# A two-layer graph network on one core: the halves of x written to DRAM in the first pass of layer 1 and loaded in the three later ones

## The chip, the core and the metric

The kernel runs on one core of one Trainium2 chip. The metric is the device time of one execution in microseconds (us). The core has a matrix engine (TensorE, PE in the profile; PEld is its weight load), a vector engine (DVE), a scalar engine (ACT), a general engine (GpSimd, POOL) and a queue engine (SyncE, SP). SP, ACT and POOL issue transfers between DRAM and on-chip memory; sixteen DMA engines carry them all.

## The reference: what is computed

There are 6250 nodes with 256 features and 100000 edges, sorted by target node. The targets are drawn as the square of a uniform number, so that low-numbered nodes have many more edges. Both layers sum the rows of the sources of a node's edges, add the node's own row, and send the result through two matrix products with ReLU. At the end x is added and each row is normalised.

```python
def _gin_agg(h, src, dst, eps, n_nodes):
    agg = jax.ops.segment_sum(h[src], dst, num_segments=n_nodes)
    return (1.0 + eps) * h + agg
...
h = _gin_agg(x, src, dst, eps1, n)
h = jax.nn.relu(h @ W1a + b1a)
h = jax.nn.relu(h @ W1b + b1b)
h = _gin_agg(h, src, dst, eps2, n)
h = jax.nn.relu(h @ W2a + b2a)
out = h @ W2b + b2b
...
x = _layernorm(x + out, axis=-1)
```

W1a is 256x512, W1b and W2a are 512x512, W2b is 512x256. Everything is float32.

## The kernel before, in words

The 6250 nodes are 49 tiles of 128 rows; the last has 106. The 100000 edges are 782 chunks of 128. A short preparation transposes the edge lists onto the partitions and makes index tables; then layer 1 writes its result `h1` (`h` in the profile) to DRAM, and layer 2 gathers from it.

**Two ways of summing edges.** In each layer the edges of most nodes are summed by *gathers*: POOL issues one indirect DMA for a chunk of 128 edges (line 461), which brings 128 rows into a buffer called `early` (in layer 2 also `late`). There are 494 such gathers in each layer. Four gathers are a piece, and the buffer holds six pieces in layer 1, so that piece i+6 can only be gathered once the sums of piece i are done. The sums are matmuls with a matrix of zeros and ones, one matmul for each gather (line 954), mostly two pieces at a time; they are copied to `split` by ACT (line 982), placed by another matmul (line 1001) and added to a tile's accumulator `acc` by DVE (line 1011). The accumulators are seeded with the tile's own rows by SP's loads (line 866) and scaled by ACT (line 883).

The lowest seven tiles (0 to 6, the *heavy* ones, 288 chunks) are done without gathers. For them layer 1 counts, for each pair of a heavy node and a source, how many edges join the two: DVE makes zero-one tiles `cb` and `ca` (lines 1532 and 1523), PE multiplies them (line 1571), and DVE adds the result to a table `at` (line 1594). Then the sums are dense products of counts with x.

**The passes over x.** `first_products` makes these products in layer 1. Their float32 precision is had by splitting x into two halves, the value rounded to the matrix engine's faster format and what is left. It goes over all of x four times: for tiles 6 and 5, 4 and 3, 2 and 1, and 0. A pass has 13 *ranges* of four tiles (the last range has one). For each range of each pass

- SP loads the range of x into a tile `raw` (`in_rows`, line 1188; 512 KB, two buffers),
- ACT rounds it into the upper half of a tile `xh` (line 1385) and copies it to PSUM in two parts (line 1392), from which DVE subtracts the upper half to make the lower one (line 1394). `xh` has two buffers,
- ACT turns the counts of each heavy tile into `cf` (line 1415), and makes and stores a 16-bit copy `ci` to DRAM for layer 2 (lines 1423 and 1428),
- PE multiplies `cf` with `xh` and adds up in one PSUM bank for each heavy tile (line 1457, four matmuls for a range and tile).

When a tile's accumulator is complete, PE transposes it (line 1047), and the two products follow (line 1086 with `w1a_s`, line 1115 with `w1b_s`); ACT evaluates the first ReLU (line 1096) and the last (line 1127), and issues the store of the result (line 1128).

**Who sets the order.** All engines run in the order in which the program is written, and a planner in the kernel (class `Plan`) sets that order: it plays the work through with assumed costs for PE, DVE and ACT, assumed times for loads (`LOAD` is 6 us), and buffers that are taken and released (`Room`). Each step of work is a Python generator that asks the planner for a buffer, for an event or for an engine, and its instructions are written at the moment the engine is granted. The order is fixed at build time; on the chip each instruction waits on semaphores for what it needs. SP's queue in layer 1 holds the loads of `raw` and of the accumulators, in the order in which the planner let them start; behind them stand the loads of layer 2.

Layer 2 has the same structure with 512 features, without the counting: it reads the 16-bit counts back (line 1243), loads `h1` as `xr`, splits it, and multiplies (line 1331).

Of the kernel before, what the change touches and what calls it, by code (L numbers as in the profile page):

```python
# [10 lines left out]
F32 = mybir.dt.float32  # L11
I32 = mybir.dt.int32
F32R = mybir.dt.float32r
# [4 lines left out]
P = 128  # L18
# [8 lines left out]
W = 10  # L27
RANGE = 4
# [133 lines left out]
GATHERS = (1.28, 1.265)  # L162
LANDINGS = (5.0, 6.0)
LOAD = 6.0
SEEDS = (6.0, 12.0)
WHOLE = 16.0
COUNTS = 12.0
# [15 lines left out]
def act(n):  # L183
    return 0.12 + 0.00083 * n
# [152 lines left out]
def tile_gin_residual_layernorm(  # L337
# [38 lines left out]
    nc = tc.nc  # L376
    N, D = x.shape
# [3 lines left out]
    NT = -(-N // P)  # L381
    NCH = -(-E // P)
    NC, taken = counted(N, E, HEAVY[0])
    STEPS, END, PASSES, FREE = steps(N, E, taken, HEAVY[0])
# [97 lines left out]
    with tc.tile_pool(name="prep", bufs=2) as prep, tc.tile_pool(  # L482
        name="prepp", bufs=2, space=bass.MemoryType.PSUM
# [30 lines left out]
        rest = E - full * P  # L514
# [44 lines left out]
        for i, c in enumerate(range(NC2, NCP, 512)):  # L559
            n = min(512, NCP - c)  # L560
# [6 lines left out]
        for g0, g1 in runs:  # L567
            c, h = groups[g0]
            n = g1 - g0
# [156 lines left out]
    def rows(t):  # L726
        return min(P, N - t * P)
# [25 lines left out]
    def ordered(ctx):  # L753
        odram = ctx.enter_context(
            tc.tile_pool(name="odram", bufs=1, space=bass.MemoryType.DRAM)
        )

        ctx.enter_context(tc.manual_schedule())

        ranges = [range(k, min(k + RANGE, NT)) for k in range(0, NT, RANGE)]  # L760
        counts = odram.tile([len(ranges), HEAVY[1], P, RANGE * P], mybir.dt.uint16, name="counts")

        def layer(number, ctx, table, width, scale, weights, ba, wide):
# [6 lines left out]
            loan = ctx.enter_context(tc.tile_pool(name=f"loan{number}", bufs=1))  # L770
# [7 lines left out]
            plan = Plan(BEGINS[number - 1], {"PE": FREES[number - 1], "DVE": FREES[number - 1],  # L778
                                             "ACT": FREES[number - 1]}, NEXT[number - 1])
# [392 lines left out]
            def whole_rows(ks):  # L1172

                return min(len(ks), N // P - ks[0])

            def in_rows(ks, to, of):

                n = whole_rows(ks)
                some = []
                if n:  # L1180
                    some.append((
                        to[:, :n],
                        of[ks[0] * P : (ks[0] + n) * P].rearrange("(k p) d -> p k d", p=P),
                    ))
                if n < len(ks):
                    some.append((to[: rows(ks[n]), n], of[ks[n] * P : N]))
                for a, b in some:
                    nc.sync.dma_start(a, b)
# [167 lines left out]
                    cleared[ts].more(sum(t >= RING for t in ts) * len(ranges))  # L1356

            def first_products():
                xh_room = Tiles(loan, [P, RANGE, 2, width], F32R, "xh", 2)
                raw_room = Tiles(loan, [P, RANGE, width], F32, "raw", 2)  # L1360
                ci_room = Tiles(loan, [P, RANGE * P], mybir.dt.uint16, "ci", 2)
                xh_of = {}
                turns = [(ts, r) for ts in PASSES for r in range(len(ranges))]
                halved = {k: Event(plan) for k in turns}
                made = {(t, r): Event(plan) for ts, r in turns for t in ts}
                factors = {}

                def loading():
                    yield ("rest", 80.0)
                    for ts, r in turns:  # L1370
                        raw = yield ("get", raw_room, 0)
                        in_rows(ranges[r], raw.tile, table)
                        token = yield ("get", xh_room, 0)
                        xh_of[ts, r] = token
                        plan.start(halving(ts, r, token.tile, raw))

                def halving(ts, r, xh, raw):
                    ks = ranges[r]
                    yield ("rest", LOAD)
                    n = whole_rows(ks)  # L1380
                    for m, js in ((P, slice(0, n)), (rows(NT - 1), slice(n, len(ks)))):
                        if js.start < js.stop:
                            c = (js.stop - js.start) * width
                            yield ("on", "ACT", act(c), 1)
                            nc.scalar.copy(xh[:m, js, 0, :], raw.tile[:m, js, :])
                            for j in range(js.start, js.stop, 2):
                                two = slice(j, min(j + 2, js.stop))
                                token = yield ("get", banks, 2)
                                c = (two.stop - j) * width
                                yield ("on", "ACT", act(c), 1)  # L1390
                                ap = bank[token.number][:m, :c].rearrange("p (k d) -> p k d", d=width)
                                nc.scalar.copy(ap, raw.tile[:m, two, :])
                                yield ("on", "DVE", dve(c), 1)
                                nc.vector.tensor_tensor(  # L1394
                                    xh[:m, two, 1, :], ap, xh[:m, two, 0, :], op=ALU.subtract
                                )
                                token.release()
                    raw.release()
                    plan.then(halved[ts, r].set)

                def factoring():
                    for ts in PASSES:
# [37 lines left out]
                def multiplying():  # L1440
                    for ts in PASSES:
                        tokens = []
                        for t in ts:
                            wanted[block_of[t]].set()
                        for r, ks in enumerate(ranges):
                            for t in ts:
                                yield ("until", made[t, r])
                            yield ("until", halved[ts, r])
                            for t in ts:
                                if r == 0:  # L1450
                                    tokens.append((yield ("get", banks, 3)))
                            yield ("on", "PE", 0.3 + 0.235 * len(ks) * len(ts), 1)
                            for i, t in enumerate(ts):
                                cf, xh = factors[t, r].tile, xh_of[ts, r].tile
                                for j, k in enumerate(ks):
                                    m = rows(k)
                                    nc.tensor.matmul(  # L1457
                                        bank[tokens[i].number][:, : 2 * width], cf[:m, j, :],
                                        xh[:m, j, :, :].rearrange("p a d -> p (a d)"),
                                        start=(k == 0), stop=(k == NT - 1),  # L1460
                                    )
                                factors[t, r].used()
                            xh_of[ts, r].release()
                        for t, token in zip(ts, tokens):
                            plan.then(plan.start, adding(t, token))

# [14 lines left out]
            def counting():  # L1481
# [1 line left out]


                F16 = mybir.dt.float16
                cb_room = Tiles(loan, [P, NT * W], F16, "cb", 10)
                ca_room = Tiles(loan, [P, BATCH, P], F16, "ca", 4)
                yield ("on", "DVE", 2.5, 4)
                si = loan.tile([P, NC], I32, tag="si", name="si")
# [399 lines left out]
```

## Time and profile before

| what | value |
|---|---|
| three timed runs | 1334.89, 1335.60, 1339.82 us (median 1335.60) |
| the profiled execution's own time | 1333.73 us |
| its span, first to last instruction | 1332.0 us |
| PE, DVE, ACT, POOL busy | 1171.7, 872.8, 603.2, 963.8 us |
| bytes moved by DMA | 305.72 MB, mean 230 GB/s |
| last gather of layer 1 / first of layer 2 issued at | 650.16 / 676.63 us |

All durations come from the profiled execution; its span is 1.7 us shorter than its own time. A line such as `L1394 DVE TENSOR_TENSOR xh<-bank,xh 128x512 ... x96 | 65.1, 684` says that the instructions of line 1394 run on DVE, write `xh` from `bank` and `xh`, stood in the span 96 times, were busy 65.1 us and took 684 ns each; behind the next bar stands how long the engine had been idle just before them, and what ended that. A queue name with a q (SPq) means the engine's issuing of a transfer, not the transfer.

### The profile page before, as it was taken

To read this page: it belongs to the slowest core of one execution; us is meant where nothing else is said; L and a number is where in the kernel's file an instruction comes from. 1 tells how busy PE (TensorE), PEld (TensorE's weight loads), DVE (VectorE), ACT (ScalarE), POOL (GpSimd) and SP (SyncE) were. 2 spreads that over 40 slices of the span, in tenths; PEclk is the share of its full clock that TensorE was granted. 3 is DMA by queue.
4 is the path that set the end of the run, shared out by engine and by line. 5 is a ranking of instruction groups with operands and counts; after the bars stand their busy time and mean duration, and the time that the engine had idled before them with its cause. 6 is when DMAs were issued, how large, how long until landed. Compare 5 with 4: busy or idle time off the path is not lost. (4 is left out here: it accounts for less than half of the span.)

```text
span 1332.0 us, 18717 instructions
## 1 busy us (share of the span) xinstructions
PE 1171.7 (88%) x6027; PEld 756.0 (57%) x6027; DVE 872.8 (66%) x2031; ACT 603.2 (45%) x1118; POOL 963.8 (72%) x1002
## 2 busy tenths in 40 slices
PE   2379888999899999878759899999989999999986
PEld 1145554655454655444436667767667766677755
DVE  7689888697897787323127668777756655653443
ACT  0213677767675763454255354334334433432222
POOL 6877777777777777777457677777777777777770
PEclk8589999999999999968879899999989999999999
DMA  3635666667676775566669889888889999877782
GB/s 103 189 119 178 182 219 198 207 199 227 207 225 188 219 239 170 151 211 193 198 228 333 296 268 310 252 278 287 289 271 309 301 310 301 289 244 240 242 244 69
DMA packets 160860, 305.72 MB, mean 230 GB/s; under 512 B 25672, under 2 KB 93150, under 8 KB 160754
## 3 DMA queue, kind: packets, MB, share of 16 engines
q0 software_dynamic: 63232, 194.31, 47.2%
q1 hardware_dynamic: 75110, 84.23, 19.3%
q10 hardware_dynamic: 22412, 25.89, 5.6%
q8 instruction: 51, 0.84, 0.3%
q14 instruction: 55, 0.45, 0.1%
HBM read 273.90 MB, written 30.44 MB: 228 GB/s over the span
## 5 line engine op out<-in xcount | busy, mean ns | idle before, releaser
L461 POOL DMA_INDIRECT early<-in_x_dram,srcs x494 | 488.9, 990 | 158.9 <-issue 127.4
L461 POOL DMA_INDIRECT early<-h,srcs x250 | 239.8, 959 | 101.4 <-issue 58.8
L461 POOL DMA_INDIRECT late<-h,srcs x244 | 232.5, 953 | 77.6 <-issue 60.2
L1011 DVE SCALAR_TENSOR_TENSOR acc<-bank,mask,acc 128x256 f32<-128x256 f32 (+1 forms) x368 | 212.8, 607 | 39.4 <-PE bank L1001 34.8
L1086 PE MATMUL bank<-zt,w2a_s 128*128 128x256 f32 (+2 forms) x864 | 181.8, 366 | 7.7 <-DVE acc L1011 6.5
L1115 PE MATMUL bank<-w1b_s,ht 128*128 128x512 f32 (+1 forms) x392 | 184.7, 599 | 1.1 <-DVE acc L1011 0.8
L1086 PEld LDWEIGHTS bank<-zt,w2a_s 128*128 128x128 f32 x864 | 154.8, 195 | 30.4 <-DVE acc L1011 6.9
L954 PE MATMUL bank<-early,sel 128*32 128x256 f32 (+1 forms) x1488 | 134.3, 475 | 32.7 <-DMA early<-h,srcs 15.3
L1331 PE MATMUL bank<-upper,cf 128*128 128x512 f32 (+1 forms) x343 | 149.2, 435 | 13.9 <-ACT upper L1220 13.5
L1331 PE MATMUL bank<-xr,cf 128*128 128x512 f32 (+1 forms) x343 | 138.2, 403 | 0.8 <-DVE xr L1225 0.8
L1594 DVE TENSOR_TENSOR at<-bank,at 128x490 f32 x174 | 115.9, 666 | 28.2 <-ACT cf L1415 14.7
L907 DVE TENSOR_TENSOR sel<-iota,slot 128x256 f32<-128x256 f32 (+2 forms) x116 | 50.6, 436 | 123.5 <-PE bank L954 119.5
L1086 PE MATMUL bank<-zt,w1a_s 128*128 128x256 f32 (+2 forms) x432 | 103.2, 389 | 13.7 <-ACT zt L1059 10.4
L1001 PE MATMUL bank<-split,to 128*128 128x256 f32 (+2 forms) x340 | 100.0, 415 | 15.6 <-ACT split L987 8.7
L1115 PEld LDWEIGHTS bank<-w1b_s,ht 128*128 128x128 f32 (+1 forms) x392 | 73.3, 191 | 70.8 <-issue 58.6
L1457 PE MATMUL bank<-xh,cf 128*128 128x512 f32 (+1 forms) x343 | 104.1, 440 | 8.7 <-DVE xh L1394 8.6
L1255 ACT CAST cf<-ci 128x512 fp32r<-128x512 uint16 (+1 forms) x91 | 53.8, 595 | 121.4 <-PE bank L1331 104.3
L1096 ACT ACTIVATE ht<-bank,b2a_s 128x256 f32<-128x256 f32 (+2 forms) x108 | 44.6, 451 | 139.5 <-PE bank L1086 137.0
L954 PEld LDWEIGHTS bank<-early,sel 128*32 128x32 f32 x1488 | 40.0, 112 | 113.4 <-issue 80.2
L1571 PE MATMUL bank<-cb,ca 128*128 128x490 f16 x288 | 87.6, 381 | 16.1 <-DVE at L1594 10.5
L1115 PE MATMUL bank<-w2b_s,ht 128*128 128x256 f32 (+1 forms) x392 | 101.5, 390 | 0.0
L1086 PEld LDWEIGHTS bank<-zt,w1a_s 128*128 128x128 f32 x432 | 81.9, 207 | 32.7 <-ACT zt L1059 14.9
(138 smaller groups left out, 1650.7 us busy)
## 6 DMA issues: line engine op xcount, KB each, us to landing
raw<-in_x_dram SPq DMA_DIRECT2D x48, 512.0 KB, 4.5
h<-h1r ACTq DMA_DIRECT2D x48, 256.0 KB, 2.5
xr<-h SPq DMA_DIRECT2D x12, 1024.0 KB, 7.3
counts<-ci ACTq DMA_DIRECT2D x84, 128.0 KB, 3.4
ci<-counts SPq DMA_DIRECT2D x84, 128.0 KB, 5.0
acc<-h SPq DMA_DIRECT2D x19, 512.0 KB, 7.5
early<-in_x_dram,srcs POOLq DMA_INDIRECT x494
acc<-in_x_dram SPq DMA_DIRECT2D x21, 256.0 KB, 3.9
```

Source lines behind the costliest of these rows:

```text
L461: nc.gpsimd.indirect_dma_start(out=rows_[:, j, :], out_offset=None, in_=table, in_offset=bass.IndirectOffsetOnAxis(ap=srcs[:, c : c + 1], ...
L907: nc.vector.tensor_tensor(sel[:, :n, :], iota[:, :SLOTS].unsqueeze(1).to_broadcast([P, n, SLOTS]), slot[:, c0 : c0 + n].unsqueeze(2).to_br ...
L954: mm = nc.tensor.matmul(pm[b * SLOTS : (b + 1) * SLOTS], sel[:, c - groups[g][0], :], rows_[:, l, :], start=(c == part[0]), stop=(c == par ...
L1001: nc.tensor.matmul(pu[:, i * width : (i + 1) * width], to[:used], split[:used, l, :], start=(once or l == 0), stop=(once or l == 1),)
L1011: nc.vector.scalar_tensor_tensor(acc[t], pu[:, i * width : (i + 1) * width], mask[:, t - lo[g], g : g + 1], acc[t], op0=ALU.mult, op1=ALU.add,
L1086: nc.tensor.matmul(ph[:, (f - o) * TILES * P : (f - o) * TILES * P + nb], wa[:, k, f * P : (f + 1) * P], zt[:, k, :nb], start=(k == 0), st ...
L1115: nc.tensor.matmul(po[:m], ht[:, f, i * P : i * P + m], wb[:, f, :], start=(f == 0), stop=(f == KH - 1),)
L1255: nc.scalar.copy(cf_token.tile[:, :n, :].rearrange("p k j -> p (k j)"), token.tile[:, : n * P],)
L1331: nc.tensor.matmul(bank[token.number][:, :width], cf[:m, j, :], of[:m, j, :], start=(j == 0 and of is upper), stop=(j == len(ks) - 1 and o ...
L1457: nc.tensor.matmul(bank[tokens[i].number][:, : 2 * width], cf[:m, j, :], xh[:m, j, :, :].rearrange("p a d -> p (a d)"), start=(k == 0), st ...
L1571: mm = nc.tensor.matmul(bank[token.number][:, : NT * W], a.tile[:, c % BATCH, :], b.tile, start=(j == 0), stop=(j == n - 1),)
L1594: nc.vector.tensor_tensor(to, bank[token[0].number][:, : NT * W].rearrange("p (k w) -> p k w", w=W), to, op=ALU.add,)
```

## The change

Only layer 1's `first_products` changes, and the sizes of its buffers. In the first pass the range's halves are stored to a new DRAM tile `halves` as soon as they are made (`keeping`), 1 MB for a range of four tiles, 8 KB in one piece for each partition. The three later passes don't load and halve x; for each range SP loads `xh` from `halves` (the `else` branch in `loading`), after the store of that range is counted as done. The planner takes 9 us for such a load and 9 + 6 us from a store's issue until a load may follow. An `xh` of the first pass has two users, the products and the store. `xh` gets three buffers instead of two, `raw` one instead of two, and the counting's `cb` eight instead of ten.

```diff
+HALVES = 9.0
...
+        halves = odram.tile([len(ranges), P, RANGE, 2, D], F32, name="halves")
...
-                xh_room = Tiles(loan, [P, RANGE, 2, width], F32R, "xh", 2)
-                raw_room = Tiles(loan, [P, RANGE, width], F32, "raw", 2)
+                xh_room = Tiles(loan, [P, RANGE, 2, width], F32R, "xh", 3)
+                raw_room = Tiles(loan, [P, RANGE, width], F32, "raw", 1)
...
+                stored = [Event(plan) for _ in ranges]
...
+                def used_rows(r):
+                    n, k = whole_rows(ranges[r]), len(ranges[r])
+                    whole = [(slice(0, P), slice(0, n))] if n else []
+                    return whole + ([(slice(0, rows(NT - 1)), slice(n, k))] if n < k else [])
...
                     for ts, r in turns:
-                        raw = yield ("get", raw_room, 0)
-                        in_rows(ranges[r], raw.tile, table)
-                        token = yield ("get", xh_room, 0)
-                        xh_of[ts, r] = token
-                        plan.start(halving(ts, r, token.tile, raw))
+                        if ts is PASSES[0]:
+                            raw = yield ("get", raw_room, 0)
+                            in_rows(ranges[r], raw.tile, table)
+                            token = yield ("get", xh_room, 0)
+                            xh_of[ts, r] = token
+                            token.users = 2
+                            plan.start(halving(ts, r, token.tile, raw))
+                        else:
+                            yield ("until", stored[r])
+                            token = yield ("get", xh_room, 0)
+                            xh_of[ts, r] = token
+                            for p, js in used_rows(r):
+                                nc.sync.dma_start(token.tile[p, js].bitcast(F32), halves[r, p, js])
+                            plan.at(plan.now + HALVES, halved[ts, r].set)
+
+                def keeping(ts, r):
+                    token = xh_of[ts, r]
+                    for p, js in used_rows(r):
+                        nc.sync.dma_start(halves[r, p, js], token.tile[p, js].bitcast(F32))
+                    yield ("rest", HALVES)
+                    token.used()
+                    yield ("rest", LOAD)
+                    stored[r].set()
...
                     plan.then(halved[ts, r].set)
+                    plan.then(plan.start, keeping(ts, r))
...
-                            xh_of[ts, r].release()
+                            (xh_of[ts, r].used if ts is PASSES[0] else xh_of[ts, r].release)()
...
-                cb_room = Tiles(loan, [P, NT * W], F16, "cb", 10)
+                cb_room = Tiles(loan, [P, NT * W], F16, "cb", 8)
```

Because the planner plays the whole layer through anew, the change also moves other work. The two places below are those that the prediction speaks of. In them `bank` is a PSUM bank, `early,sel` are the sums of gathers, `xh,cf` the products of a pass, `w1a_s` and `w1b_s` the two products of a finished tile, `split,to` the placing of sums; x4 stands for that many instructions in a row, and a number behind a name tells one buffer from another.

First PE, where the fourth pass (tile 0) begins. Before:

```order
L1457 MATMUL bank0_486<-xh_5027,cf_5445 128x512 x4
L1115 MATMUL bank5_491<-w1b_s_474,ht_5349 128x512 x2
L1115 MATMUL bank1_487<-w1b_s_474,ht_5349 128x512 x4
L954 MATMUL bank3_489<-early_83,sel_5312 32x256 x4
L954 MATMUL bank3_489<-early_83,sel_5378 32x256 x4
L1457 MATMUL bank0_486<-xh_5447,cf_5455 128x512 x4
L1457 MATMUL bank0_486<-xh_5461,cf_5473 128x512 x4
L954 MATMUL bank3_489<-early_83,sel_5378 32x256 x8
L1001 MATMUL bank5_491<-split_5560,to_5313 128x256
L1001 MATMUL bank5_491<-split_5560,to_5379 128x256
```

The same place on PE in the changed kernel (its line 1486 is line 1457 of before, 956 is 954, 1088 is 1086, 1117 is 1115, 1003 is 1001):

```order
L1486 MATMUL bank6_493<-xh_4626,cf_5215 128x512 x4
L1088 MATMUL bank2_489<-zt_5167,w1a_s_474 128x256 x4
L1486 MATMUL bank6_493<-xh_4684,cf_5225 128x512 x4
L956 MATMUL bank7_494<-early_83,sel_5119 32x256 x8
L1486 MATMUL bank6_493<-xh_4734,cf_5236 128x512 x4
L1003 MATMUL bank4_491<-split_5270,to_5051 128x256
L1003 MATMUL bank4_491<-split_5270,to_5120 128x256
L1117 MATMUL bank5_492<-w1b_s_475,ht_5098 128x512 x2
L1088 MATMUL bank0_487<-zt_5167,w1a_s_474 128x256 x4
L1486 MATMUL bank6_493<-xh_5227,cf_5279 128x512 x4
L1117 MATMUL bank1_488<-w1b_s_475,ht_5098 128x512 x2
L956 MATMUL bank2_489<-early_83,sel_5190 32x256 x8
```

The ranges of a pass stand closer together among the sums of gathers. Counted over the whole of PE's order, between the first and the last row of a pass stood 88, 80, 72 and 56 sum matmuls (passes one to four), and now stand 104, 56, 64 and 32. The fourth pass began with 80 of the layer's 494 sum matmuls still to come and ended with 24; now it begins with 96 and ends with 64. POOL's order is the same in both kernels, and so is PE's from the layer's last eight sums on.

Second SP, in the first pass (`acc` are loads of accumulator seeds). Before:

```order
L1188 DMA raw_1378<-in_x_dram 128x4x256
L1188 DMA raw_1562<-in_x_dram 128x4x256
L866 DMA acc_1566<-in_x_dram 128x2x256
L1188 DMA raw_1654<-in_x_dram 128x4x256
L1188 DMA raw_1771<-in_x_dram 128x4x256
L866 DMA acc_1862<-in_x_dram 128x2x256
```

And in the changed kernel (1190 is 1188 of before, 868 is 866):

```order
L1190 DMA raw_1516<-in_x_dram 128x4x256
L1399 DMA halves_469<-xh_1370 128x2048
L1190 DMA raw_1682<-in_x_dram 128x4x256
L1399 DMA halves_469<-xh_1518 128x2048
L868 DMA acc_1693<-in_x_dram 128x2x256
L868 DMA acc_1819<-in_x_dram 128x2x256
L1190 DMA raw_1880<-in_x_dram 128x4x256
L1399 DMA halves_469<-xh_1684 128x2048
```

A store of halves now stands behind each load of the following range, and the seeds' loads stand behind both.

## Prediction

> **What bounds the kernel now.** I read the page first, for each engine's share of the span:
>
> ```profile
> PE 1171.7 (88%) x6027; PEld 756.0 (57%) x6027; DVE 872.8 (66%) x2031; ACT 603.2 (45%) x1118; POOL 963.8 (72%) x1002
> ```
>
> No engine is full over the whole span, so the two layers have to be looked at apart. The table of busy time by stretch has for each engine its busy us and its instructions; the last three columns are the granted clock of TensorE, the share of the DMA engines, and GB/s:
>
> ```profile
> core 0: us, PE busy (x) PEld busy (x) DVE busy (x) ACT busy (x) POOL busy (x), PEclk, DMA share, GB/s
> 100.00:150.00 50.00, 47.12 (x226) 27.18 (x225) 44.97 (x101) 21.73 (x40) 37.68 (x40) 0.94 0.60 184
> 500.00:550.00 50.00, 46.33 (x233) 25.64 (x233) 33.70 (x83) 14.38 (x28) 37.83 (x40) 1.00 0.51 155
> 550.00:600.00 50.00, 39.46 (x171) 20.62 (x170) 13.12 (x24) 30.19 (x51) 37.92 (x40) 0.80 0.66 200
> 600.00:652.00 52.00, 38.46 (x181) 22.32 (x180) 15.74 (x31) 19.88 (x39) 38.80 (x41) 0.84 0.69 217
> 700.00:1332.00 632.00, 598.02 (x3268) 428.48 (x3267) 389.70 (x786) 237.43 (x456) 454.42 (x476) 0.98 0.83 270
> ```
>
> In layer 1 POOL does 40 gathers in every 50 us, one each 1.25 us, whether DVE is busy 45 us or 13 us beside it. From 700 us on PE is the full engine (598 of 632 us). What POOL waited for up to 700 us, and its last steps of layer 1 and first of layer 2 in the timeline:
>
> ```profile
> POOL early L461 <- issue: 129.2, 424, 0.3
> POOL early L461 <- DMA h<-h1r: 25.5, 1, 25.5
> POOL early L461 <- PE bank L954: 7.2, 13, 1.5
> ...
> 650.16 0.95 POOL L461 DMA_INDIRECT early<-in_x_dram,srcs  x1 [0.30 <-issue]
> 676.63 1.13 POOL L461 DMA_INDIRECT early<-h,srcs  x1 [25.53 <-DMA h<-h1r]
> ```
>
> The 129.2 us are the 0.3 us between any two gathers. Waits for sums to free a buffer are 7.2 us in 13 cases, of which 13 x 0.3 = 3.9 us would stand there anyhow: POOL lost 3.3 us in 494 gathers. So layer 1 lasts as long as POOL needs to issue its gathers, up to 651 us, and then the 25.5 us from the last gather through the last tiles to the store of `h1`. Whatever moves the last gather or this tail moves the end by as much; PE, DVE and ACT matter in layer 1 only where they make a sum too late. Layer 2's order is unchanged.
>
> **What is removed.** The halving in the passes, by groups up to 650 us, with the queue's wait that stands before the loads and the `cb` that loses two buffers:
>
> ```profile
> L1385 ACT CAST xh<-raw 128x1024 fp32r<-128x1024 f32 x48 | 50.0, 1043 | 5.8 <-ACT ci L1423 2.5 <-PE bank L1457 1.2 <-ACT h1r L1127 1.2
> L1392 ACT COPY bank<-raw 128x512 f32<-128x512 f32 x96 | 55.8, 589 | 20.4 <-DVE xh L1394 6.5 <-DVE at L1594 6.2 <-ACT h1r L1127 3.6
> L1394 DVE TENSOR_TENSOR xh<-bank,xh 128x512 fp32r<-128x512 f32 x96 | 65.1, 684 | 49.9 <-ACT bank L1392 49.5
> L1532 DVE TENSOR_SCALAR cb<-numbers,spot 128x490 f16<-128x490 f16 x288 | 89.4, 352 | 8.4 <-PE bank L1571 8.3
> SPq L1188 <- ACT bank L1392: 285.8, 39, 26.0
> ```
>
> Three of four passes lose it: ACT 36 x 1.04 + 72 x 0.59 = 80 us, DVE 72 x 0.684 = 49 us. All of it lay beside POOL's gathers, which were not waiting for it, so its direct worth is nothing but those 3.3 us, at most. Two of their rows, the first and the last of the four above 0.5 us, and the first product of a pass:
>
> ```profile
> 108.53 0.94 POOL L461 DMA_INDIRECT early<-in_x_dram,srcs  x1 [0.75 <-PE bank L954]
> 234.73 0.94 POOL L461 DMA_INDIRECT early<-in_x_dram,srcs  x1 [1.16 <-PE bank L954]
> L1457 PE MATMUL bank<-xh,cf x343: 387/394/988, 144.7 to 630.8; 128*128 128x512 f32 x168, 106*128 106x512 f32 x4
> ```
>
> The first pass spans 88 sums, 88 x 1.25 = 110 us from 144.7, that is to about 255 us. The stalls lie before or in it, and this pass keeps its halving. I take 0 of the 3.3 us as gained (bounds -3.3 and 0).
>
> **What is added in the first pass.** Thirteen stores of halves, 1 MB each but the last. On SP a store waits for the last subtraction of its range, and behind it stand the next load of `raw` and the loads of seeds, for which ACT's scaling and then DVE's adding of sums wait. SP already stood 285.8 us behind ACT's copies of a range (last row of the fence above), a subtraction of 0.68 us earlier, and POOL lost its 3.3 us in spite of that; so I take 0, and at most +4 us, a doubling of the old stalls. The single `raw` and the eight `cb` I put at 0 too, inside that bound: the order stretches the pass from 88 to 104 sums, and DVE waited 8.3 us for `cb` over the whole layer, without POOL standing still for it.
>
> **What is added in the later passes.** Three times 12.8 MB of loads instead of 6.4 MB. Passes two and three span 56 and 64 sums, 70 and 80 us. Pass four spans 32, which is 40 us, and ran in 77.8 us before (first row of PE, last row), with the transfers in a stretch without loads of x, those ACT issued during the pass, and the nearest load of 1 MB, layer 2's:
>
> ```profile
> 553.23 0.64 PE L954 MATMUL bank<-early,sel 128*32 128x256 f32 x8 [1.03 <-DMA early<-in_x_dram,srcs]
> 553.80 0.96 PE L1457 MATMUL bank<-xh,cf 128*128 128x512 f32 x3
> 630.84 0.80 PE L1457 MATMUL bank<-xh,cf 106*128 106x512 f32 x1
> ...
> q0 software_dynamic: 1923, 5.22, 35.3%
> q10 hardware_dynamic: 720, 1.31, 7.6%
> ...
> q10 hardware_dynamic: 2736, 3.18, 11.1%
> ...
> xr<-h SPq DMA_DIRECT2D x12, 1024.0 KB, 7.3
> ```
>
> The gathers (q0) take 35.3% of the engines' time. ACT's stores (q10) took 11.1% of 81 us, 9.0 us of all engines. At 1.31 MB for 7.6% of 50 us, q10 moves 345 GB/s of engine time. Three ranges fit into `xh` ahead of the pass; the other nine and the short one are 9.65 MB, 28 us. A pass of T us then needs 0.353 T + 9.0 + 28 = T, so T = 57 us (estimate, with the engines full). It would run 17 us behind the plan. At the other end, a load that lands in 7.3 us with three in flight gives a range each (7.3 + 1.9) / 3 = 3.1 us (1.9 us for four products of 0.394 us and their start), 40 us for the pass, and no lag.
>
> How much lag POOL forgives can be read off the sum at 553.23 us, which waited for its gathers: 80 sums come after it, so its last gather went out at 650.16 - 80 x 1.25 = 550.2 us and landed 3 us later. The buffer of the first of its two pieces is needed again 17 gathers on, at 571.4 us. So a sum may be 17.5 us late before POOL stops. A lag of 17 us just fits; with slower landings it doesn't quite. I take +2 us, bounds 0 and +10 (a pass of 67 us). Passes two and three by the same sum, with the gathers and 28 us plus their share of stores, need about as much as the fourth and have 70 us: 0, at most +3.
>
> **The tail.** The end of layer 1 on PE, and the clock there:
>
> ```profile
> 649.25 3.47 PE L1086 MATMUL bank<-zt,w1a_s 128*128 128x128 f32 x16 [5.47 <-ACT zt L1059]
> 653.22 3.70 PE L1115 MATMUL bank<-w1b_s,ht 128*128 128x512 f32 x8
> 656.85 1.07 PE L954 MATMUL bank<-early,sel 128*32 128x256 f32 x16
> 661.32 3.84 PE L1086 MATMUL bank<-zt,w1a_s 128*128 128x128 f32 x32
> 664.99 7.03 PE L1115 MATMUL bank<-w1b_s,ht 128*128 128x512 f32 x16
> ...
> 649.20:652.70 3.50, 3.45 (x20) 3.33 (x24) 0.00 (x0) 0.63 (x2) 1.60 (x2) 0.56 0.98 291
> 661.00:665.00 4.00, 3.93 (x35) 3.69 (x35) 0.00 (x0) 2.51 (x8) 0.00 (x0) 1.00 0.00 0
> 665.00:672.10 7.10, 7.02 (x18) 2.85 (x16) 0.73 (x2) 1.25 (x3) 0.00 (x0) 1.00 0.00 0
> ```
>
> The last sums ran at 656.85 us, though their gathers had landed by about 650.16 + 3 = 653.2 us: eight matmuls of `w1b_s` stood before them. Now the pass is over with 64 sums to come instead of 24, the loads for layer 2 that waited for its end leave earlier, and PE has less to do at the end. That is worth 0 to 3.6 us; I take -1, since the last rows are the same. The other end of this term is the clock, below: +8.7.
>
> At the granted clock of 0.56, 16 matmuls of line 1086 took 3.47 us (0.217 each); at 1.00, 32 took 3.84 us (0.120). A half clock in the tail would add 0.8 x (3.84 + 7.03) = 8.7 us. [...] The trace has both clocks within 12 us, so it leaves open which comes.
>
> The sum is 0 + 0 + 0 + 2 - 1 = +1 us on the profiled execution's 1333.73 us. The median of the runs shown is 1335.60, 1.9 us above it; on the median I forecast **1336.6 us**.
>
> **The rivals.** Half a per cent, 6.7 us, is about what a measurement of this kernel can tell from no change.
>
> *The fourth pass waits for its loads (slower).* If the halves come in so slowly that the pass needs 70 us instead of 40, sums are 30 us late, POOL stands 30 - 17.5 = 12.5 us, and nothing later gives that back: 1348 us. It decides from a pass of 57.5 us on, and passes the half per cent at 64 us. For it: the estimate of 57 us is at the edge, takes the engines as full, and leaves out that ACT's stores and copies of counts are in step with the pass. Against it: layer 2 runs at a DMA share of 0.83 for 632 us with PE nearly full.
>
> *The tail meets the half clock (slower).* 1335.6 + 8.7 + 1, about 1345 us. For it: PE's clock was 0.80 and 0.84 in the stretches after 550 us, where it already had less to do. Against it: the tail itself had 1.00.
>
> *Gathers get faster (faster).* Two more rows, the gathers of layer 1 as a group and POOL up to 100 us:
>
> ```profile
> L461 POOL DMA_INDIRECT early<-in_x_dram,srcs x494 | 488.9, 990 | 158.9 <-issue 127.4
> 8.00:100.00 92.00, 72.04 (x64) 0.70 0.46 141
> ```
>
> At the 0.946 us of 500 to 550 us, 494 gathers would take 467.3 us; they took 21.6 us more, 11.5 of them before 100 us, where nothing changes. If the other 10 us came from DVE's work and all went, together with the 3.3 us, the time would be 1322 us. Against it: DVE loses 49 us of its work, not all, and POOL's 40 gathers took 37.7 us where DVE was busiest.
>
> **How the numbers follow.** The forecast, within 0.5% of before, gets 0.62, since POOL hides what is removed and mostly what is added. Slower gets 0.31: 0.20 for the fourth pass and 0.11 for the clock. Faster gets 0.07. The forecast's own terms reach from 1331 to 1342. The range takes in the clock's 1345 and most of the fourth pass's 1348, and below half of the way to the fast rival: 1329 to 1349 us.
>
> **What would show it.** The last gather of layer 1 should still go out at about 650 us, with POOL's waits on sums under 10 us, and the first of layer 2 at 675 to 678 us. The fourth pass should take 50 to 60 us on PE, its products waiting for DMA instead of DVE. ACT should lose 80 us and DVE 49. I am wrong if POOL's 494 gathers take over 10 us longer or shorter, or if layer 2, whose order is the same, takes another time from its first gather on.

## The result, and the profile after

In runs side by side the changed kernel took 1341.53 us (median of 20, 1333.19 to 1348.53) and the kernel before 1333.83 us (20, 1328.66 to 1339.82): a ratio of 1.0054, 95% interval 1.0035 to 1.0073. A second measurement of the same kernel (experiment e9) gave 1339.56 against 1334.44 us, 1.0038 (1.0025 to 1.0052). It is slower by 5 to 8 us, at the edge of what a measurement can tell from no change; the forecast was +1. The ratios leave out disturbed executions, which only the second chip of the experiments had. The profiled executions took 1337.89 us (after) and 1340.02 us (e9), spans of 1336.1 and 1338.3.

Lines of the changed file stand 1 to 29 lower: gathers 462, seeds' loads 868 and scaling 885, sums 956, adding 1013, transposes 1049, products of the tail 1088 and 1117, halves' stores 1399 and loads 1393, `ci` 1452, products of the passes 1486.

The page, engines and queues (q1 is SP's):

```profile
PE 1169.0 (87%) x6027; PEld 754.3 (56%) x6027; DVE 830.5 (62%) x1956; ACT 530.6 (40%) x1004; POOL 968.7 (73%) x1002
q0 software_dynamic: 63232, 194.31, 46.1%
q1 hardware_dynamic: 63122, 116.23, 25.0%
```

ACT lost 73 us and DVE 42, and the program moves 337.71 MB instead of 305.72. POOL's waits up to 700 us, the last gather of layer 1, and the first of layer 2:

```profile
POOL early L462 <- issue: 130.2, 427, 0.3
POOL early L462 <- DMA h<-h1r: 20.2, 1, 20.2
POOL early L462 <- PE bank L956: 9.0, 8, 3.0
...
656.83 0.95 POOL L462 DMA_INDIRECT early<-in_x_dram,srcs  x1 [0.30 <-issue]
677.99 1.20 POOL L462 DMA_INDIRECT early<-h,srcs  x1 [20.21 <-DMA h<-h1r]
```

The last gather goes out 6.7 us later than before. The first gather started 0.5 later (8.77 to 9.29), and the group of 494 is busy 491.6 instead of 488.9 us, +2.7. The rest is stalls. These three rows are nearly all of them, in the first pass:

```profile
180.74 0.95 POOL L462 DMA_INDIRECT early<-in_x_dram,srcs  x1 [1.99 <-PE bank L956]
193.37 0.95 POOL L462 DMA_INDIRECT early<-in_x_dram,srcs  x1 [2.41 <-PE bank L956]
206.10 0.95 POOL L462 DMA_INDIRECT early<-in_x_dram,srcs  x1 [3.02 <-PE bank L956]
```

Less the 0.3 us that stand before any gather, they cost 1.7 + 2.1 + 2.7 = 6.5 us, where before lost 3.3. What made the second one late can be followed backwards on PE, DVE, ACT and SP:

```profile
189.95 1.12 PE L1049 MATMUL bank<-ident,acc 128*128 128x128 f32 x4 [2.66 <-DVE acc L1013]
191.96 1.94 PE L956 MATMUL bank<-early,sel 128*32 128x256 f32 x16 [0.90 <-ACT zt L1061]
...
188.44 0.67 DVE L1623 TENSOR_TENSOR at<-bank,at 128x490 f32 x1 [2.23 <-ACT at L1466]
...
185.79 0.72 ACT L885 ACTIVATE acc<-acc,e 128x512 f32<-128x512 f32 x1 [1.52 <-DMA acc<-in_x_dram]
...
176.71 0.34 SPq L1399 DMA_DIRECT2D halves<-xh  x1
177.17 14.29 SPq L868 DMA_DIRECT2D acc<-in_x_dram  x2
```

SP issued a 1 MB store and, 0.5 us later, a seed's load behind it (the second load of the last row went out 14 us on). ACT stood for that seed until 185.8 us, 8.6 us after the issue; in the median a seed's load took 3.9 us before. ACT's next work on the counting's table (`at`, line 1466) came after it, DVE stood 2.23 us for that, and DVE's adding at 189.03 stood behind. PE's transposes waited for that adding, and the sums that free POOL's buffer (191.96) stood behind them. The other two stalls were not followed back like this, but PE lost time behind its waits as well: from 190 to 196 us the granted clock was 0.50 (1.00 from 176.7 to 186 us, and 1.00 from 150 to 215 us in the run e1 below), and these 16 sums took 1.94 us, where the 16 at 179.79 us took 1.07.

The fourth pass, the groups of its products: of before, as the prediction has them, 553.8 to 630.8. Of after:

```profile
L1486 PE MATMUL bank<-xh,cf x49: 387/397/988, 546.8 to 605.0; 128*128 128x512 f32 x48, 106*128 106x512 f32 x1
550.00:600.00 50.00, 34.73 (x152) 19.36 (x151) 8.10 (x18) 17.28 (x32) 37.88 (x40) 0.85 0.93 350
```

It took 58.2 us between its first and its last product (59 with the last one's own time) with the DMA engines 93% busy, close to the 57 us worked out in advance. POOL still made its 40 gathers in that stretch. New, and not named in the prediction, is what ACT waits for between 60 and 690 us; after, and below it before:

```profile
ACT ci L1452 <- DMA counts<-ci: 67.1, 30, 7.9
ACT acc L885 <- DMA acc<-in_x_dram: 15.8, 7, 5.8
```

```profile
ACT acc L883 <- DMA acc<-in_x_dram: 1.5, 1, 1.5
ACT ci L1423 <- DMA counts<-ci: 0.8, 1, 0.8
```

There are two `ci` buffers, and ACT now waits up to 7.9 us for one of the 128 KB stores that empty them; before, such a store landed 3.4 us after its issue in the median. It looks like the cause; the experiments below don't bear that out.

### The profile page after: what moved, and what is told of

Its sections match the earlier page's. It is cut to its first block, busy times and chain, and to the rows that moved or that the text cites. A ratio compares the mean times of both kernels' runs of the same rounds, so it can differ in the third digit from the quotient of the medians.

```text
span 1336.1 us, 18618 instructions
## 1 busy us (share of the span) xinstructions
PE 1169.0 (87%) x6027; PEld 754.3 (56%) x6027; DVE 830.5 (62%) x1956; ACT 530.6 (40%) x1004; POOL 968.7 (73%) x1002
## 2 busy tenths in 40 slices
DMA packets 148871, 337.71 MB, mean 253 GB/s; under 512 B 25866, under 2 KB 74594, under 8 KB 142622
## 4 chain that ended last, share of the span: by engine, by line
PE 51%; DMA 21%; DVE 9%; ACT 6%; issue 4%; POOL 4%; DVEq 1%; ACTq 1%; POOLq 0%; SPq 0%
PE bank L1088 16%; DMA counts<-ci 10%; PE bank L1117 10%; PE bank L1333 8%; PE bank L956 8%; DMA early<-h,srcs 4%; POOL early L462 4%; PE bank L1003 4%; DMA acc<-in_x_dram 3%; DVE at L1623 2%; DVE acc L1013 2%; PE bank L1049 2%; PE bank L1600 2%; ACT ci L1452 2%; PE bank L1486 1%
## 5 line engine op out<-in xcount | busy, mean ns | idle before, releaser
L462 POOL DMA_INDIRECT early<-in_x_dram,srcs x494 | 491.6, 995 | 162.9 <-issue 128.0
L1117 PE MATMUL bank<-w1b_s,ht 128*128 128x512 f32 (+1 forms) x392 | 187.4, 606 | 0.0
L1257 ACT CAST cf<-ci 128x512 fp32r<-128x512 uint16 (+1 forms) x91 | 53.9, 595 | 122.8 <-PE bank L1333 102.5
L1561 DVE TENSOR_SCALAR cb<-numbers,spot 128x490 f16<-128x490 f16 x288 | 90.2, 355 | 10.3 <-PE bank L1600 9.7
```

The costliest lines, as they stand in the source:

```text
L462: nc.gpsimd.indirect_dma_start(out=rows_[:, j, :], out_offset=None, in_=table, in_offset=bass.IndirectOffsetOnAxis(ap=srcs[:, c : c + 1], ...
L1117: nc.tensor.matmul(po[:m], ht[:, f, i * P : i * P + m], wb[:, f, :], start=(f == 0), stop=(f == KH - 1),)
L1257: nc.scalar.copy(cf_token.tile[:, :n, :].rearrange("p k j -> p (k j)"), token.tile[:, : n * P],)
L1561: made = nc.vector.tensor_scalar(token.tile, numbers, spot[:, c : c + 1], None, op0=ALU.is_equal)
```

## The experiments

Theory A: the order and the buffers cost nothing; the added bytes do, and the stores of the first pass through POOL's stalls. Theory B: the new order or the smaller buffers (`raw`, `cb`) cost it, whatever the bytes. Inside A, the loads could cost through the fourth pass or through ACT's wait for `ci`. e1 to e4 ran on one chip, e5 to e8 on a second, e9 to e12 on a third.

**e1, both directions thinned.** The order is the same word for word; stores and loads of halves move the first of four tiles.

```diff
 for p, js in used_rows(r):
+    js = slice(js.start, js.start + 1)
     nc.sync.dma_start(halves[r, p, js], token.tile[p, js].bitcast(F32))
...
-xh[:m, j, :, :].rearrange("p a d -> p (a d)"),
+xh[:m, j if ts is PASSES[0] else 0, :, :].rearrange("p a d -> p (a d)"),
```

The same slice stands in the loop of the loads.

> The instructions and their order on every engine are those of the changed kernel; only the first of a range's four tiles of halves is stored (256 KB instead of 1 MB) and loaded, and the later passes multiply that one tile four times, so their sums aren't those of the reference. Theory 1, the bytes: the added transfers make everything on the DMA engines land later, ACT waits for the stores of counts (67 us in the changed kernel, under 1 us before) and sums come late. Then ACT's wait for counts falls under 15 us, POOL's waits on sums under 4 us above their floor, and the time to 1328 to 1334 us. Theory 2, the order and the buffers: one buffer of raw, eight of cb and the new places of the passes make sums late, whatever is moved. Then POOL's stalls at 180 to 206 us stay and the time stays at 1339 to 1343 us.

Measured: 1333.90 against 1333.89 us, 1.0006 (0.9991 to 1.0022). The interval lies below both of the changed kernel's; but e9's was taken on another chip, and the chip of the first isn't on record. POOL's waits, and the only two stalls left after the first 20 us, in a profile of the fastest of this run's twelve executions (1329.60 us):

```profile
POOL early L462 <- PE bank L956: 3.9, 9, 1.0
...
179.36 0.94 POOL L462 DMA_INDIRECT early<-in_x_dram,srcs  x1 [1.00 <-PE bank L956]
200.62 0.94 POOL L462 DMA_INDIRECT early<-in_x_dram,srcs  x1 [0.77 <-PE bank L956]
```

Here ACT scaled the same seeds at 182.78 us without a wait, behind a store of 256 KB, where after did so at 185.79. Of the profiles with whole stores and this order, e2 and e9 have such a wait of ACT for a seed between 150 and 215 us too, 1.0 and 2.0 us. Against after, the sums ahead of that scaling run 1.4 us earlier (178.42, 179.79 there), those behind it 3.1 us earlier (188.81, 191.96 there). With the order, the single `raw` and eight `cb` of the changed kernel and a quarter of its bytes, the time is that of before: theory B falls.

**e2, loads alone thinned.** The stores are whole; only the slice in the loop of the loads and the product's index are changed.

> As the run before, but the stores keep their full 1 MB; only the loads of the three later passes are cut to a quarter. If the loss comes from the loads, this is as fast as with both cut, 1328 to 1334 us. If it comes from the first pass and its stores, POOL still stalls by about 6 us at 180 to 206 us and the time is 3 to 5 us above that of the run with both cut. Theory 2 expects 1339 to 1343 us for both.

Measured: 1336.11 us, 1.0025 (1.0009 to 1.0042). The stalls of the first pass are back, at the same places as in the changed kernel:

```profile
181.33 0.95 POOL L462 DMA_INDIRECT early<-in_x_dram,srcs  x1 [2.20 <-PE bank L956]
193.44 0.94 POOL L462 DMA_INDIRECT early<-in_x_dram,srcs  x1 [2.18 <-PE bank L956]
205.56 1.08 POOL L462 DMA_INDIRECT early<-in_x_dram,srcs  x1 [2.44 <-PE bank L956]
```

Between e1 and e2 only the stores' bytes differ. They bring 5.9 us of stalls against 1.2, and the last gather at 656.19 instead of 650.42 us. The medians differ by 2.2 us, less than the 3 to 5 expected, and the ratios' intervals overlap. The means of the twelve executions of each differ by 2.9 us (95% interval about 0.6 to 5.0).

**e3, a third `ci` buffer.** The planner still counts two, so the order stays; a new last argument of `Tiles` gives the real number of buffers, and ACT's store has one more to land.

```diff
-ci_room = Tiles(loan, [P, RANGE * P], mybir.dt.uint16, "ci", 2)
+ci_room = Tiles(loan, [P, RANGE * P], mybir.dt.uint16, "ci", 2, 3)
```

> The changed kernel with a third buffer for the 16-bit counts that ACT stores; the planner still counts two, so the order is unchanged. Theory 1a: ACT's wait for these stores is the way in which the transfers reach the sums. Then that wait falls from 67 us to under 25 us and the time by 3 to 7 us, to 1335 to 1338 us. Theory 1b: the wait is slack, and the sums are late in the first pass for other reasons (seeds behind the stores on SP, DVE). Then the wait falls as much and the time stays within 2 us of 1341 us.

Measured: 1336.75 us, 1.0020 (1.0001 to 1.0040), and on ACT:

```profile
ACT ci L1453 <- DMA counts<-ci: 22.1, 14, 5.0
```

The wait fell by 45 us; POOL's stalls of the first pass stayed (5.9 us), and the last gather went out at 655.84. The time lies where theory 1a (the wait is the path) had it. But the ratio's interval overlaps with both of the unaltered kernel's, which didn't run on this chip, so a gain isn't shown. What e3 does show is the bytes: with all of them it took 3.5 us more than e1 in the mean (about 1.3 to 5.9), in the same order and on the same chip.

**e4, the ceiling.** The later passes neither halve nor load: they multiply the first range's halves each time, and nothing is stored. The planner makes an order of its own.

```diff
-token = yield ("get", xh_room, 0)
-xh_of[ts, r] = token
-for p, js in used_rows(r):
-    nc.sync.dma_start(token.tile[p, js].bitcast(F32), halves[r, p, js])
...
+xh_of[ts, r] = xh_of[PASSES[0], 0]
...
-plan.then(plan.start, keeping(ts, r))
...
```

> The ceiling: the later passes neither halve nor load; they multiply the halves of the first range again and again (kept in their buffer), so their sums aren't those of the reference, and nothing is stored. The planner makes a new order. If POOL's gathers bound layer 1, the most that any cheaper way to the halves can bring is the stalls of 3 us and some 5 us of the tail: 1325 to 1334 us. If ACT and DVE were a second bound hidden by the first, the time falls below 1320 us.

Measured: 1332.79 us, 0.9993 (0.9979 to 1.0006). If halving in three passes cost nothing at all, the kernel would win 1 us, not told from nothing. So, in the order that this planner makes, the idea had nothing to win here, and no version of it was tried further.

**e5 to e8, on a chip where both kernels take longer.** e5 thins the loads of the fourth pass alone, e6 those of passes two and three, e7 is the changed kernel unaltered, e8 has eight heavy tiles in layer 1.

> The changed kernel, in its own order, with only the fourth pass's loads cut to a quarter of their bytes (its sums are then not those of the reference). The loads cost some 5 us of the median in all (1341.5 with them, 1336.1 with all cut). If they cost them in the fourth pass, as the prediction had it, this run is at 1335 to 1338 us. If they cost them in the second and third, it stays at 1339 to 1343 us.

> The complement: only the second and third pass's loads are cut to a quarter (sums not those of the reference). If the fourth pass is where the loads cost their time, 1339 to 1343 us; if the second and third are, 1335 to 1338 us.

> The changed kernel as it is, for a second profile and its time beside these runs: 1339 to 1344 us. Its first profile, at 1337.9 us, lay below the median. A profile nearer to the median or above it should show the last gather of layer 1 later than 656.8 us by what it is longer: by stalls of POOL after 550 us if the fourth pass is late (theory of the prediction), or by longer ones at 180 to 260 us if the first pass is.

> If POOL's gathers bound layer 1, what ACT and DVE no longer do is worth something only as room for work that takes gathers off POOL. Here the eighth tile of layer 1 is done by counts and products too (layer 2 still has seven): 474 gathers instead of 494, 25 us less for POOL. If the sums keep up, 1315 to 1322 us. If PE, 44 to 50 us busy in each 50 us up to 550 us, is the next bound, the gain is 0 to 12 us, 1330 to 1341 us.

On this chip the kernel before took 1613.67 us (29 runs, 1591.46 to 1626.59), so only ratios to it mean anything here: e5 0.9894 (0.9842 to 0.9946), e6 0.9908 (0.9876 to 0.9939), e7 0.9904 (0.9858 to 0.9949), e8 1.0056 (1.0011 to 1.0101). The medians over all runs of e7 and of before, 1610.80 and 1613.67, are nearer to each other than the ratio. The expected microseconds don't apply, and the three thinned or whole variants aren't told apart. e7's gathers and POOL's waits over the span:

```profile
L462 POOL DMA_INDIRECT early<-in_x_dram,srcs x494 | 490.4, 993 | 302.3 <-issue 131.3 <-PE bank L956 102.5 <-PE bank L1600 21.8
...
POOL early L462 <- PE bank L956: 126.6, 26, 11.3
POOL early L462 <- remote: 38.5, 17, 3.1
POOL late L462 <- PE bank L956: 38.2, 12, 5.0
```

A gather takes as long as on the other chips (993 against 995 ns), but POOL stands still for sums, 102.5 us in layer 1. POOL isn't the bound there, and the changed kernel is not slower there. That fits a change whose worth depends on whether gathers hide the halving; it was not isolated.

**e9 to e12, the same questions on a third chip.** e9 is the changed kernel unaltered, as the measure.

> The changed kernel, unaltered, as the measure for the three that follow. On a chip where the kernel before takes about 1334 us: a ratio of 1.004 to 1.007, ACT waiting some 60 us for the stores of counts, POOL stalling near 180, 193 and 206 us. On a chip where the kernel before takes over 1600 us, as in the runs before: a ratio of 0.990 to 1.000.

Measured: 1339.56 us, 1.0038 (1.0025 to 1.0052), POOL's stalls near 180, 193 and 206 us again (6.3 us), ACT 63.4 us for `ci`, the last gather at 655.98.

**e10, the fourth pass's loads alone.**

```diff
 for p, js in used_rows(r):
+    if ts is PASSES[-1]:
+        js = slice(js.start, js.start + 1)
...
```

The products of that pass take the first tile four times.

> Only the fourth pass loads a quarter of the halves (it multiplies one tile four times, so its output differs). If the loads cost time in the fourth pass (its 58 us against 40), on the usual chip some 4 us less than the changed kernel, a ratio to before of about 1.003, the fourth pass under 50 us. If the loads of the second and third pass cost it, through ACT's wait for the stores of counts, the same time as the changed kernel, 1.005, and ACT's wait for counts stays at two thirds of 67 us or more.

Measured: 1339.67 us, 1.0051 (1.0030 to 1.0072). The pass, in e9 and in e10:

```profile
L1486 PE MATMUL bank<-xh,cf x49: 387/397/987, 547.4 to 602.6; 128*128 128x512 f32 x48, 106*128 106x512 f32 x1
```

```profile
L1488 PE MATMUL bank<-xh,cf x49: 387/397/796, 546.5 to 589.3; 128*128 128x512 f32 x48, 106*128 106x512 f32 x1
```

The pass got 12 us shorter (42.8 instead of 55.2), and the kernel not at all. The fourth pass's lag lies inside POOL's slack. ACT's wait for `ci` fell to 38.0 us, more than expected.

**e11, the loads of passes two and three alone.** The same edit with `ts in PASSES[1:-1]`.

> Only the second and third pass load a quarter of the halves (they multiply one tile four times, so the output differs). If the fourth pass alone costs time: as the changed kernel, 1.005. If the second and third pass do: some 4 us less, 1.003 or below, and ACT's wait for the stores of counts falls below 30 us.

Measured: 1339.03 us, 1.0031 (1.0016 to 1.0047). ACT's wait fell from 63.4 to 26.9 us, and the kernel took no less time that could be told: the ratio lies between what the two theories expected, the medians of e9 and e11 differ by 0.5 us. So as far as can be told, the part of this wait that went was covered, too. The profiled execution (span 1343.5) is one of the slower ones, with stalls from 108 us on, ahead of where the edit acts.

**e12, eight heavy tiles.** Twenty gathers fewer, and one tile more in the passes.

```diff
-HEAVY = (7, 7)
+HEAVY = (8, 7)
```

> The changed kernel with eight instead of seven of layer 1's tiles' sources held in counts, so that 20 gathers fewer stand on POOL. If POOL's gathers alone bound layer 1: 20 x 1.25 = 25 us less than the changed kernel, about 1316 us, ratio to before 0.985. If the products of the passes, which grow by as much work, bound it now: no faster than the changed kernel, or slower, with POOL waiting for sums.

Measured: 1359.82 us, 1.0196 (1.0172 to 1.0220). POOL's waits and its last gather, and the products of the passes from 500 us on:

```profile
POOL early L462 <- DMA acc<-h: 55.0, 1, 55.0
POOL early L462 <- PE bank L956: 17.5, 11, 9.8
...
640.79 0.94 POOL L462 DMA_INDIRECT early<-in_x_dram,srcs  x1 [0.30 <-issue]
...
L1486 PE MATMUL bank<-xh,cf x108: 387/395/988, 501.9 to 672.2; 128*128 128x512 f32 x104, 106*128 106x512 f32 x4
```

The gathers were done 15 us earlier than in e9, but the passes ended only after 672 us and layer 2 began at 696.72. POOL is the bound of layer 1 with seven heavy tiles, but not by far: what a tile more adds to the passes exceeds what it takes from POOL's queue, as the second of the two expectations had it.

The profiled executions beside each other, in us. Stalls are the part over 0.3 us of POOL's waits for sums between 100 and 240 us; "pass four" is first to last product; "wait" is what the tail's last sums stood for their gathers, "x32" the 32 matmuls of line 1088 behind them, and "layer 2" the time from its first gather to the end of the span:

| kernel | ratio | stalls | last gather | pass four | wait | x32 | first gather, layer 2 | layer 2 |
|---|---|---|---|---|---|---|---|
| before | 1 | 3.2 | 650.16 | 77.0 | 0 | 3.84 | 676.63 | 655.4 |
| after | 1.0054 | 6.5 | 656.83 | 58.2 | 1.36 | 3.84 | 677.99 | 658.1 |
| e9 (the same) | 1.0038 | 6.3 | 655.98 | 55.2 | 3.39 | 6.00 | 680.84 | 657.5 |
| e1 | 1.0006 | 1.2 | 650.42 | 44.6 | 4.51 | 5.42 | 674.02 | 653.6 |
| e2 | 1.0025 | 5.9 | 656.19 | 45.5 | 4.42 | 5.16 | 679.62 | 652.5 |
| e10 | 1.0051 | 5.9 | 657.72 | 42.8 | 4.23 | 5.64 | 682.20 | 653.0 |
| e11 | 1.0031 | 12.8 | 662.28 | 59.7 | 3.33 | 6.07 | 687.15 | 656.4 |

On the first and third chip every kernel with whole stores and 494 gathers (e3 as well) has its last gather at 655.8 us or later; the one with thin stores has it where before has it. One case doesn't fit so simply: e4, which stores nothing but runs in an order of its own, had 6.3 us of such stalls, spread from 129 to 206 us, and its last gather at 655.38. So the stalls of a pass hang on the order too, and the stores are shown to be their cause only for the order that after, e1 and e2 share. Nor do such stalls alone make the kernel slower: e4 takes no longer than before, with a layer 2 of 651.8 us.

## Why the prediction was right, and where it was not

The forecast of +1 us was a change too small to tell from none, and at +7.7 and +5.1 us it is nearly that: one lies just over, one under the half per cent (6.7 us) that the prediction drew. Luck helped. In after's profile the last gather comes 6.7 us later, the tail gives 5.3 us back, and layer 2 takes 2.7 us more; in e9's these are 5.8, 1.6 and 2.1. Neither rival that the prediction had for a slower kernel explains the loss: the fourth pass cost nothing that can be told, the half clock in the tail 2.2 us at most. The median of before, 1333.83 us over 20 runs, also lies 1.8 us below that of the three runs on which the forecast was built. And the bounds of the terms, without the clock, add up to 1329 and 1353 us, not to the 1331 and 1342 that the prediction names.

*Removed halving: 0.* Right. e4, which takes it out for nothing in return, is at 0.9993, in its own order. The 3.3 us of old stalls were not gained by it either: the changed kernel has more.

*Stores of the first pass: 0, at most +4.* This is the term that was mis-sized. The mechanism stood there (SP's queue, the seeds behind the stores, DVE's adding), and 0 was taken because SP's wait of 285.8 us had cost only 3.3 us. But that wait was for ACT's copies and made hardly a seed late: ACT stood once for a seed, 1.5 us, between 60 and 690 us (15.8 us after). Now a seed's load itself comes late behind the bytes of a store (ACT could go on 8.6 us after its issue, where such a load took 3.9 us in the median before), and the transposes and sums stand behind it. The new entry in the queue alone isn't the cause, as e1 has it too, with 1.2 us of stalls. Measured: stalls of 6.5 and 6.3 us instead of 3.2, so +3 against before, near the bound, and 5 against e1, which has the same order. With e1's result, this is the one cost that has both its place in the trace and an experiment that takes it away, in this order; how much of it reaches the end of the kernel is open, as e4 shows.

*Passes two and three: 0, at most +3; fourth pass: +2, at most +10.* The pass itself was worked out well, 57 us against 59 and 56. Its cost was not +2 but nothing that can be told: e10 shortens it by 12 us for no gain. The slack of 17.5 us held; the one wait there of after that exceeded 0.3 us was 0.39 us, at 617.77. For passes two and three e11 says the same, although its wait on ACT was overlooked. All loads together may still cost something, 1.0025 with a quarter of them against 1.0038 and 1.0054 with all; but the intervals overlap, and e3, with all of them on e2's chip, is at 1.0020. A place for it would be layer 2, as the last point below says. What part of the 5 to 8 us is left to them stays open.

*The tail: -1.* Its size depends on the execution: 20.2 us in after's profile, 23.9 in e9's, against 25.5. They win 5.3 and 1.6 us, both more than the 1 us forecast, and the first more than its bound of 3.6.

*Rival: the fourth pass waits (1348 us).* It did not happen. The pass reached the 57.5 us from which this rival was to decide, and POOL didn't stop.

*Rival: the tail meets the half clock (1345 us).* It did, in part. The tail in e9, and the busy time in two stretches of it (the third column from the end is the granted clock):

```profile
659.24 1.08 PE L956 MATMUL bank<-early,sel 128*32 128x256 f32 x8 [3.39 <-DMA early<-in_x_dram,srcs]
663.77 6.00 PE L1088 MATMUL bank<-zt,w1a_s 128*128 128x128 f32 x32
669.61 7.03 PE L1117 MATMUL bank<-w1b_s,ht 128*128 128x512 f32 x16
...
663.80:669.60 5.80, 5.80 (x32) 5.80 (x33) 0.00 (x0) 2.23 (x7) 0.00 (x0) 0.61 0.00 0
669.60:676.60 7.00, 7.00 (x18) 2.86 (x16) 0.69 (x1) 1.26 (x3) 0.00 (x0) 1.00 0.00 0
```

PE, finished sooner, stood 3.39 us for the last gathers, and the next 32 matmuls took 6.00 us at a clock of 0.61 instead of 3.84 at 1.00. In the table each wait of 3.3 us or more has such a row behind it (5.16 to 6.07 us), and the waits of 0 and 1.36 us have 3.84. So a PE that is finished sooner did lose time behind its wait, but 1.3 to 2.2 us in these 32 matmuls, and no run shows the prediction's 8.7 us. That estimate put all of 10.9 us of matmuls at the half clock; in e9 the clock was 1.00 again in the 16 of line 1117, and they took 7.03 us, as before. What makes the clock fall and rise was not isolated.

*Rival: gathers get faster (1322 us).* It did not happen: 995 ns for one instead of 990, with 42 us of DVE's work gone.

*What would have shown it.* The last gather at about 650 us came 6.7 later; the first pass's stalls, the mis-sized term, are about half of that. POOL's wait on sums stayed under 10 us (9.0), but over 8 cases instead of 13, so less of it was the ordinary 0.3: a total over all cases hid what three rows showed. ACT lost 73 us, not 80, and DVE 42, not 49: the halving on ACT itself went as worked out (108.9 us of it before, 27.4 after), and where the other groups got longer was not followed. Layer 2, in the same order, took 658.1 us from its first gather on instead of 655.4, which the prediction named as a sign of being wrong. The profiles of kernels that share this order there fall in two groups: those whose fourth pass loads everything, halves or x, took 655.4 to 658.1 us (before, after, e9, e11, and e3 with 656.4), those in which it loads a quarter or nothing took 651.8 to 653.6 (e1, e2, e4, e10). One stall differs: between 40 and 130 us after the first gather POOL stands up to 2.7 to 4.1 us for a sum in the first group, and nowhere over 1.6 us in the second. So the fourth pass's loads may cost time in layer 2. It isn't shown: e10, in the second group, isn't faster than e9 in the median, and the profiles of e1 and e10 are of the fastest of their executions.

## What to carry to other kernels

Work that lies beside the engine that bounds a stage can be worth nothing when it is removed (e4, without the halving of three passes: 0.9993), and what replaces it is not free (after: 1.0054): ask of each new transfer which small load stands behind it in its queue, how many bytes that load then has ahead of it, and who waits for it. Here the same entry cost POOL 1.2 us of stalls with 256 KB and 5.9 us with 1 MB. A long wait at the head of a queue, 285.8 us on SP with 3.3 us lost on POOL, said little on what a new entry there costs, as what was queued behind came in time all the same. And a wait that grows from 1 to 67 us can be mostly slack: only an experiment that takes it away tells whether it is on the path; e11 took 36 us of it without a gain that could be told.

## What was not expected

Small stores kept their engine waiting beside the bulk transfers of another queue: for its 128 KB stores of counts, which landed after 3.4 us in the median before, ACT waited up to 7.9 us each and 67.1 us in all after, and 5.3 us in all in e2, whose loads move a quarter of the bytes. One of the three chips of the experiments took 21% longer for the unaltered kernel before (1613.67 against 1333.89 us), with gathers of the same duration (993 ns) and long idle times between them; the cause is not known. Twenty gathers fewer made the kernel 2% slower (e12), as the passes end last then.
